# Forget gate's token products in seven blocks of half its columns, with the last steps' weights split into freed places

## The chip, the cores and the metric

The kernel runs on one core of a Trainium2 chip. What counts is the device time of one execution in microseconds (us), lower being better; it is given as the median of several runs.

## The reference

The input x holds 32 slices of 128 tokens with 512 features, all in fp32. Two layers follow one another, each adding to x what a feed-forward part makes of a conditioning part. The first layer's parts are a mixture of experts with a shared expert, and a selection of weights by slice. The second layer's conditioning part sends tokens to 16 experts by a hash of their ids and multiplies the result by a sigmoid gate; its output z enters a gated recurrence over the 32 slices:

```python
def step(c, xt):
    ft = sigmoid(xt @ wf.T + c @ uf.T + bf)
    it = sigmoid(xt @ wi.T + c @ ui.T + bi)
    gt = tanh(xt @ wc.T + c @ uc.T + bc)
    return ft * c + it * gt
# 32 steps, c is 128 x 512; then
h = tanh(z @ wo.T + c_final @ uo.T + bo)
x = x + h
```

All w and u are 512 x 512. The change concerns this recurrence and the step into the last line.

## The kernel before

Every matrix product keeps fp32 accuracy by three products of parts. `split` makes a high part in the format fp32r (a copy on ScalarE, ACT) and a low part (a subtraction on VectorE, DVE) of a tile; `mm3` runs, for each 128 rows of the contraction, high x high, high x low and low x high into one PSUM bank. So a product of 128 x 512 by 512 x 512 is 12 matmuls of 512 moving columns.

A step t of the recurrence has three parts. `from_c` multiplies the state, turned and split into `cT`, by uc, ui and uf: 36 matmuls into three banks of the pool `ps_g`. `gate` adds bias or token product to a bank (DVE, L1720), takes tanh or sigmoid (ACT, L1721); `new_c` forms the new state on DVE (L1726, L1728). `turn` then transposes it on TensorE (tile ptC, L1647) and splits it. The chain from the end of `from_c` of f over the gate, the new state, ptC and the split of `cT` is what the next step waits for; TensorE fills that time with token products of later steps, which need no state.

The token products of c and i are made for two steps at once by Winograd's form of Strassen's product: the tokens of the two steps in two halves of the contraction are A11, A12 (first step) and A21, A22 (second), the weights B11, B21 (wc) and B12, B22 (wi). Seven blocks of 6 matmuls take the place of eight, from the sums S1 to S4 of tokens (`sums_z`, DVE L1637 to L1641) and T1 to T4 of weights. `first_of_pair(n)` runs five blocks and their additions (L1690 to L1695) ahead of the even step 2n, `second_i(n)` one (additions L1705, L1706) and `second_c(n)` one (L1711) ahead of the odd step. A block takes one of the three banks of the pool `ps_b`. In the first two steps `plain` makes the products without sums; there the right half is made from B11, T1 and B22, since T1 has taken the place of B12.

The forget gate's token product is made by `plain` for every step, 12 matmuls of 512 into the same `ps_g` bank to which `from_c` of that step adds; they follow `second_i` in odd steps and `turn` in even ones. Its bias is added by `gate`.

The tokens of step t + 3 are prepared in step t by `gate_y`: a gather of y by GpSimd (POOL, L1587) and a load of r by the queue SP, a sigmoid, a product (L1612), transposes (tile ptF, L1620), a copy, a store of z to DRAM for the last stage, and splits into the tile z. One tile z of two holds the tokens and sums of a pair.

A planner places the instructions of each engine: it takes them in the order written, but where the written one would have to wait, by its own costs, it takes a later one. `issue_after`, `behind` and `queue_behind` hold an instruction back behind another of its engine. A tile in a place used before waits until the old tile's last reader is done.

After the loop the output products come: for 8 groups g of 512 tokens, `unit(g, o)` multiplies wo by the group's z (tile poF, 12 matmuls of 512, four units a group). uo by the final state gives cu (48 matmuls of 128 columns). `result` adds cu, takes tanh, adds x1 and stores. In the old kernel wo is split in step 28, the first group's z and uo behind the loop, while the last step runs.

Pools that matter: `wx_p` holds the split w, `uci` uc and ui, `uf_p` uf, `zp` the tiles z, `zop` raw weights and the sums of blocks, `op` what the last stage loads.

Of the kernel before, what the change touches and what calls it, by code (L numbers as in the profile page):

```python
# [8 lines left out]
F32 = mybir.dt.float32  # L9
# [40 lines left out]
def tile_kernel(ctx: ExitStack, tc: tile.TileContext, a: dict, out: bass.AP):  # L50
# [106 lines left out]
    hl = const.tile([P, KD, NB], F32, name="hl")  # L157
# [18 lines left out]
    with ExitStack() as sa:  # L176
# [653 lines left out]
        new_i = po_p.tile([P, NB], I32, name="new_i")  # L830
        ones = po_p.tile([P, P], F32, name="ones2")
# [734 lines left out]
    with sf:  # L1566
# [35 lines left out]
        zp = sf.enter_context(tc.tile_pool(name="zp", bufs=2, **kw))  # L1602

        zA, zS, zts = {}, {}, {}

        def gate_y(b):
# [6 lines left out]
            if j == 0:  # L1613
                z = zp.tile([P, 2 * KD * D], FR, tag="z", name=f"z_{n}")
                zA[n] = z[:, : KD * D].rearrange("p (j h k q) -> p j h k q", j=2, h=2, k=KD)
                zS[n] = z[:, KD * D :].rearrange("p (s h k q) -> p s h k q", s=4, h=2, k=K2)
                zts[n] = first_p.tile([P, 2, KD, P], F32, tag="cT0", name=f"zt_{n}")
# [5 lines left out]
            zt = zts[n][:, j]  # L1623
            if b < LEAD:
                split(zA[n][:, j, 0], zA[n][:, j, 1], pt)
# [3 lines left out]
            if b >= LEAD:  # L1629
                split(zA[n][:, j, 0], zA[n][:, j, 1], zt)  # L1630

        def sums_z(n):
# [3 lines left out]
            s = gp.tile([P, 2, K2, P], F32, tag="sz", name=f"sz_{n}")  # L1636
# [7 lines left out]
        def turn(c, t):  # L1644
            pt = ps_c.tile([P, KD, P], F32, tag="t", name=f"ptC_{t}")
            for k in range(KD):
                nc.tensor.transpose(pt[:, k, :], c[:, bass.ts(k, P)], ident)  # L1647
# [6 lines left out]

        def block(which, w, n):

            s = {"A11": (0, 0), "A12": (0, 1), "A22": (1, 1)}.get(which)
            if s is None:
                left = zS[n][:, int(which[1]) - 1]
            else:  # L1660
                left = zA[n][:, s[0], :, s[1] * K2 : (s[1] + 1) * K2]
            ps = ps_b.tile([P, D], F32, tag="b", name=f"p{which}_{n}")
            mm3(ps, lambda h, k: left[:, h, k, :], lambda h, k: wt[w][:, h, bass.ts(k, D)], K2)
            return ps

        def plain(t, ps, which, start, stop):
# [5 lines left out]
                "f": ((0, "f0"), (1, "f1")),  # L1672
# [3 lines left out]
            for m, (half, w) in enumerate(todo):  # L1676
                z = zA[n][:, j, :, half * K2 : (half + 1) * K2]
# [6 lines left out]
        half_done, made = {}, []  # L1684

        def first_of_pair(n):

            first, second, c1 = (zop.tile([P, 2, D], F32, tag="raw", name=f"{x}_{n}") for x in ("ta", "tb", "pa"))
            p1, u, v = first[:, 0], first[:, 1], second[:, 0]
            nc.vector.tensor_tensor(p1, block("A11", "B11", n), bias["c"], ALU.add)  # L1690
# [27 lines left out]
        def gate(t, n, ps, v, more):  # L1718
            v[n] = gp.tile([P, D], F32, tag="v" + n, name=f"v_{n}_{t}")
# [5 lines left out]
        def new_c(t, v, c):  # L1725
# [5 lines left out]

        wt = {
            n: wx_p.tile([P, 2, K2 * D], FR, tag="w" + n, name=f"w{n}_hl")
            for n in ("T4", "T3", "T2", "f1", "B22", "T1", "B21", "B11", "f0")
# [26 lines left out]
        for n in "cif":  # L1761
            from_c(0, n, ps, cT, True, False)


        f01 = zp.tile([P, 2 * KD * D], F32, tag="z", name="raw_wf")
        f01 = [f01[:, bass.ts(h, K2 * D)] for h in range(2)]
        with tc.issue_after(first_got):
            for h in range(2):
                nc.gpsimd.dma_start(out=f01[h], in_=a["wf"].rearrange("p k n -> p (k n)")[:, bass.ts(h, K2 * D)])
# [3 lines left out]
        with behind(first_z):  # L1773
            for h in range(2):
                split_part(f"f{h}", f01[h])
# [4 lines left out]
        def rest_of_weights():  # L1780
# [6 lines left out]
            split_part("T4", c1)  # L1787

        cT_next = cT
        for t in range(NB):  # L1790
# [3 lines left out]
            if t == 0:  # L1794
# [3 lines left out]
                with tc.issue_after(done):  # L1798
                    plain(0, ps, "f", False, True)
                for n in "cif":  # L1800
                    gate(t, n, ps, v, more[n])
            else:
                for n in "cif":
# [8 lines left out]
            if t == 0:  # L1812
# [5 lines left out]
                plain(1, ps, "f", True, False)  # L1818
            elif t < NB - 1:
                if odd:  # L1820
                    second_i(n)
                    plain(t + 1, ps, "f", True, False)
                else:
                    first_of_pair(n)
                cT_next = turn(c, t + 1)
                if odd:
                    second_c(n)
                else:
                    plain(t + 1, ps, "f", True, False)
            else:  # L1830
                cT_next = turn(c, t + 1)
            for b in (2, 3) if t == 0 else (t + 3,) if t + 3 < NB else ():
                gate_y(b)
                if b + LEAD < NB:
                    get_y(b + LEAD)
                if b % 2:
# [184 lines left out]
```

## Time and profile before

| what | us |
|---|---|
| median of 3 runs (2414.24 to 2421.07) | 2416.92 |
| the profiled execution | 2416.54 |
| its span in the profile | 2414.9 |
| TensorE busy (PE) | 2393.2 |
| VectorE busy (DVE) | 1485.1 |
| ScalarE busy (ACT) | 1079.8 |
| the recurrence with its start | about 1776 to 2315 |
| one pair of steps in it | 33.2 |
| from its last product to the second group of outputs | 2315 to 2333 |

The granted TensorE clock was 0.999 of full speed. In the profile PE is TensorE's matmuls, PEld its weight loads, which overlap them; L and a number is a line of the kernel, and matmuls of `mm3` all have line 95, so they are told apart by their tiles: ps_c, ps_i and ps_f are the banks of the three gates, pA and pS blocks of tokens and of token sums, poF the output products. A matmul's length in the timeline includes its way through the array, so that neighbours overlap; from one start to the next is its slot. In a row of waits, the engine and tile that waited stand left of the arrow and what ended the wait right of it.

### The profile page before, as it was taken

Reading aid. Unit: us, or ns where it says so; the run is one execution under the profiler, and the core shown is the slowest. Engines: PE = TensorE matmul, PEld = TensorE weight load, DVE = VectorE, ACT = ScalarE, POOL = GpSimd, SP = SyncE. Lnnn points to the kernel's source line nnn. Section 1 sums busy time; section 2 is a strip of 40 time slices with the busy share of each in tenths; the row PEclk is TensorE's granted clock in tenths of the full one; section 3 lists DMA queues with packets and bytes.
Section 4 is the critical chain, followed back from the end, with each engine's and each line's share of the span. In section 5 each row is a group of like instructions: output and inputs, shape, how many; then the busy total and the mean of one; then the engine's idle time right before and its main releaser. Section 6 shows DMA issues by size and latency. Waiting matters only on the chain.

```text
span 2414.9 us, 36797 instructions
## 1 busy us (share of the span) xinstructions
PE 2393.2 (99%) x12792; PEld 2028.2 (84%) x12792; DVE 1485.1 (61%) x2548; ACT 1079.8 (45%) x1897; POOL 417.4 (17%) x461
## 2 busy tenths in 40 slices
PE   9999999999999999999999999999999999999999
PEld 6788888888887888888888889999988888888887
DVE  8797644456567445446455477776756666666664
ACT  5544633343223545445455466666643223223242
POOL 1000022222233233323222120000010000000012
PEclk9999999999999999999999999999999999999999
DMA  6445555457564334343243287677642111111165
GB/s 219 150 131 170 184 171 167 151 188 254 175 222 156 128 128 130 106 132 110 86 151 125 90 297 253 226 224 233 196 156 63 49 44 53 49 44 49 53 238 181
DMA packets 196383, 357.93 MB, mean 148 GB/s; under 512 B 37665, under 2 KB 70481, under 8 KB 193633
## 3 DMA queue, kind: packets, MB, share of 16 engines
q1 hardware_dynamic: 148224, 258.57, 32.0%
q0 software_dynamic: 36448, 75.95, 10.6%
q10 hardware_dynamic: 11520, 20.98, 2.4%
q8 instruction: 107, 1.75, 0.3%
q14 instruction: 84, 0.68, 0.1%
HBM read 377.08 MB, written 91.80 MB: 194 GB/s over the span
## 4 chain that ended last, share of the span: by engine, by line
PE 78%; DMA 1%; DVE 1%; issue 1%; ACT 1%; ACTq 0%; POOL 0%; DVEq 0%; POOLq 0%
PE phD L95 7%; PE poD L95 7%; PE po L95 7%; PE ps_f L95 7%; PE p L95 6%; PE pb L95 4%; PE ps_i L95 4%; PE ps_c L95 4%; PE poF L95 3%; PE pS L95 3%; PE pv L95 3%; PE acc L95 3%; PE pA L95 2%; PE pur L95 2%; PE por L95 2%
## 5 line engine op out<-in xcount | busy, mean ns | idle before, releaser
L65 DVE TENSOR_TENSOR wD<-rawD,wD 128x1024 fp32r<-128x1024 f32 x128 | 156.5, 1229 | 77.6 <-ACT wD L64 77.5
L95 PE MATMUL p<-xhl,swu 128*128 128x512 f32 x768 | 190.6, 400 | 5.7 <-ACT xhl L64 5.7
L95 PE MATMUL p<-xhl,kept_u 128*128 128x512 f32 x768 | 184.6, 394 | 1.2 <-DVE kept_u L65 0.7
L95 PEld LDWEIGHTS phD<-xe,wD 128*128 128x128 f32 x1536 | 183.2, 188 | 1.3
L95 PE MATMUL phD<-xe,wD 128*128 128x256 f32 x1536 | 183.5, 279 | 0.0
L95 PE MATMUL poD<-wD,hD 128*128 128x512 f32 x768 | 181.5, 392 | 0.0
L95 PEld LDWEIGHTS p<-xhl,swu 128*128 128x128 f32 x768 | 145.7, 192 | 36.8 <-ACT xhl L64 5.9
L95 PEld LDWEIGHTS p<-xhl,kept_u 128*128 128x128 f32 x768 | 141.9, 188 | 31.3 <-DVE kept_u L65 1.1
L95 PEld LDWEIGHTS poD<-wD,hD 128*128 128x128 f32 x768 | 141.9, 188 | 28.3
L64 ACT CAST wD<-rawD 128x1024 fp32r<-128x1024 f32 x128 | 133.6, 1047 | 52.7 <-PE poD L95 31.0
L305 POOL DMA_INDIRECT xg<-in_x_rows_dram,blk_t x71 | 68.1, 960 | 439.0 <-PE ptx L315 242.0
L1587 POOL DMA_INDIRECT y<-res_d,gat_i x32 | 35.8, 1118 | 472.9 <-DVE r L1612 394.3
L95 PE MATMUL pur<-r,xb 128*128 x792 | 110.6, 288 | 3.3 <-issue 1.5
L65 DVE TENSOR_TENSOR xb<-ptx,xb 128x512 fp32r<-128x512 f32 x68 | 47.0, 691 | 106.1 <-ACT xb L64 102.7
L95 PE MATMUL por<-r,hbr 128*128 x396 | 107.6, 407 | 0.5 <-ACT hbr L64 0.5
L95 PEld LDWEIGHTS pur<-r,xb 128*128 128x128 f32 x792 | 98.6, 188 | 5.6 <-issue 2.7
L95 PE MATMUL ps_c<-uc_hl,cT 128*128 128x512 f32 x384 | 96.3, 399 | 0.0
L95 PE MATMUL pb<-rT,Wo_hl 128*128 128x256 f32 x768 | 94.7, 281 | 0.3 <-DVE rT L65 0.2
L95 PE MATMUL ps_f<-wf_hl,z 128*128 128x512 f32 x384 | 94.5, 394 | 0.0
L95 PE MATMUL acc<-kept_d,as 128*128 128x512 f32 x384 | 93.6, 392 | 0.4 <-DVE as L65 0.2
L844 POOL DMA_INDIRECT o<-o_d,s_i x64 | 64.7, 1011 | 168.0 <-PE pth L864 82.9
L95 PE MATMUL pv<-w_recept_hl,xr 128*128 128x512 f32 x384 | 93.7, 392 | 0.0
(1048 smaller groups left out, 5130.5 us busy)
## 6 DMA issues: line engine op xcount, KB each, us to landing
rawD<-in_w_key_dram SPq DMA_DIRECT2D x64, 512.0 KB
rawD<-in_w_value_dram SPq DMA_DIRECT2D x64, 512.0 KB
swr<-in_sw_dram SPq DMA_DIRECT2D x120, 256.0 KB
o_d<-obr SPq DMA_DIRECT2D x66, 256.0 KB
rraw<-in_rw_dram SPq DMA_DIRECT2D x32, 256.0 KB
xc<-in_x_dram SPq DMA_DIRECT2D x32, 256.0 KB
hid_d<-o ACTq DMA_DIRECT2D x32, 256.0 KB
xh_d<-xc SPq DMA_DIRECT2D x32, 256.0 KB
```

The costliest lines, as they stand in the source:

```text
L64: first = nc.scalar.copy(hi, src).ins
L65: done = nc.vector.tensor_tensor(lo, src, hi.bitcast(F32), ALU.subtract).ins
L95: done = nc.tensor.matmul(ps, lhsT=left(hl, k), rhs=right(hr, k), start=start and k + n == 0, stop=stop and 3 * k + n == last,)
L305: nc.gpsimd.indirect_dma_start(out=xg[i], out_offset=None, in_=a["x_rows"], in_offset=bass.IndirectOffsetOnAxis(ap=blk_t[:, i : i + 1], ax ...
L844: nc.gpsimd.indirect_dma_start(out=o[n], out_offset=None, in_=o_d, in_offset=bass.IndirectOffsetOnAxis(ap=idx[:, b : b + 1], axis=0),)
L1587: got = nc.gpsimd.indirect_dma_start(out=y, out_offset=None, in_=res_d, in_offset=bass.IndirectOffsetOnAxis(ap=gat_i[:, b : b + 1], axis=0),)
```

## The change

The forget gate's token product also goes by seven blocks, but within one gate: wf is cut into 2 x 2 parts of 256 rows by 256 columns, the tokens of two steps into 2 x 2 parts as before, so the same sums S1 to S4 serve, and the blocks have 256 moving columns. They hold for steps 4 to 31. Steps 0 to 3 use `plain_f`, five half-products of 6 matmuls of 256. The product no longer shares a bank with `from_c`: it goes through `ps_b`, and DVE adds it up in a tile `fs[t]`, into which `gate` then adds `from_c`'s bank. A pair's seven blocks are run as two (`f_start(n + 1)`, in the odd step before the pair), three (`f_first`, behind `turn` of the even step), one (`f_second`, behind `second_i`) and one (`f_third`, behind `second_c`). The adds of `f_start` and `f_second` are queued behind the split of `cT`, those of `f_first` behind the new state.

Places move: the split parts of wf stand in one tile `wf` that begins 64 bytes off a multiple of 512, as the moving operands of the expert stage do (tile xe there, phD the product); the tile z holds tokens alone and the sums have one place `zs`, which raw wf has first; the sums' scratch is the y tile of the odd step, so the gather of the next y comes behind `sums_z`; `hl`, an early tile, leaves the pool `const`.

In the last steps wo is split in step 29 into the places of B11 and B21 (`wo0`), the first group's z in step 30 into those of T1 and T2, and uo behind the final state into uc's. The first group's units use these; wo is split once more, into `wo1`, for the other groups. The transposes of the final state are queued behind `unit(0, 1)`. The second group's z and the first x1 are loaded into ui's place.

```diff
-    hl = const.tile([P, KD, NB], F32, name="hl")
...
+        hl = po_p.tile([P, KD, NB], F32, name="hl")
...
-        zA, zS, zts = {}, {}, {}
+        sz = sf.enter_context(ExitStack())
+        zp = sz.enter_context(tc.tile_pool(name="zp", bufs=2, **kw))
+
+
+        zA, zS, zts, a21 = {}, {}, {}, []
+        BLOCKS = {(0, 0): 0, (0, 1): 1, (1, 1): 2}
+
+        def tokens(n, j, half):
+
+            return zA[n][:, BLOCKS[j, half]] if (j, half) in BLOCKS else a21[0]
...
-                z = zp.tile([P, 2 * KD * D], FR, tag="z", name=f"z_{n}")
+                zA[n] = zp.tile([P, 3, 2, K2, P], FR, tag="z", name=f"z_{n}")
...
-            s = gp.tile([P, 2, K2, P], F32, tag="sz", name=f"sz_{n}")
+            zS[n] = zp.tile([P, 4, 2, K2, P], FR, tag="zs", bufs=1, name=f"zs_{n}")
+            s = spare[2 * n + 1].rearrange("p (s k q) -> p s k q", s=2, k=K2)
...
-            for k in range(KD):
-                nc.tensor.transpose(pt[:, k, :], c[:, bass.ts(k, P)], ident)
+            turned_c[:] = [
+                nc.tensor.transpose(pt[:, k, :], c[:, bass.ts(k, P)], ident).ins for k in range(KD)
+            ]
...
+        def blocks_f(n, *todo):
+
+            ps = ps_b.tile([P, 2, HD], F32, tag="b", name=f"pf{todo[0][0]}_{n}")
+            for i, (which, w) in enumerate(todo):
+                left = left_of(which, n)
+                mm3(ps[:, i], lambda h, k: left[:, h, k, :], lambda h, k: wf[w][:, h, k, :], K2)
+            return ps
...
+        def f_tile(t):
+            pool, tag = (gp, "vf") if t % 2 or t == 0 else (first_p, "c0")
+            fs[t] = pool.tile([P, D], F32, tag=tag, name=f"v_f_{t}")
+            return fs[t][:, :HD], fs[t][:, HD:]
+
+        def plain_f(t):
+            n, j = divmod(t, 2)
+            f_tile(t)
+            ps = ps_b.tile([P, 2, HD], F32, tag="b", name=f"pf_{t}")
+            for i, todo in enumerate((((0, "B11"), (1, "B21")), ((0, "B11"), (0, "T1"), (1, "B22")))):
+                for m, (half, w) in enumerate(todo):
+                    z = tokens(n, j, half)
+                    mm3(
+                        ps[:, i], lambda h, k: z[:, h, k, :], lambda h, k: wf[w][:, h, k, :], K2,
+                        m == 0, m == len(todo) - 1,
+                    )
+            return nc.vector.tensor_tensor(fs[t], ps.rearrange("p i n -> p (i n)"), bias["f"], ALU.add).ins
+
+        def f_start(n):
+
+            f1, p1 = f_tile(2 * n)
+            ps = blocks_f(n, ("A11", "B11"), ("A12", "B21"))
+            return [
+                nc.vector.tensor_tensor(p1, ps[:, 0], bias["f"][:, :HD], ALU.add).ins,
+                nc.vector.tensor_tensor(f1, ps[:, 1], p1, ALU.add).ins,
+            ]
+
+        def f_first(n, room):
+
+            u, v = room[:, :HD], room[:, HD:]
+            p1 = fs[2 * n][:, HD:]
+            ps = blocks_f(n, ("S1", "T1"), ("S2", "T2"))
+            last = blocks_f(n, ("S4", "B22"))
+            with tc.issue_after(made[0]):
+                nc.vector.tensor_tensor(v, ps[:, 0], bias["f"][:, HD:], ALU.add)
+                nc.vector.tensor_tensor(u, ps[:, 1], p1, ALU.add)
+                nc.vector.tensor_tensor(v, v, u, ALU.add)
+                nc.vector.tensor_tensor(p1, last[:, 0], v, ALU.add)
+            f_done[n] = u, v
+
+        def f_second(n):
+            f1, f2 = f_tile(2 * n + 1)
+            u, v = f_done.pop(n)
+            ps = blocks_f(n, ("S3", "T3"))
+            adds = [
+                nc.vector.tensor_tensor(u, ps[:, 0], u, ALU.add).ins,
+                nc.vector.tensor_tensor(f2, ps[:, 0], v, ALU.add).ins,
+            ]
+            return (f1, u), adds
+
+        def f_third(n, f1, u):
+            nc.vector.tensor_tensor(f1, blocks_f(n, ("A22", "T4"))[:, 0], u, ALU.add)
...
+            rooms[n] = second[:, 1]
...
-            v[n] = gp.tile([P, D], F32, tag="v" + n, name=f"v_{n}_{t}")
+            v[n] = fs.pop(t) if n == "f" else gp.tile([P, D], F32, tag="v" + n, name=f"v_{n}_{t}")
...
+        names = ("T4", "T3", "T2", "B22", "T1", "B21", "B11")
+        f_all = shifted(wx_p, len(names) * K2 * D, tag="wf", name="wf_hl")
+        f_all = f_all.rearrange("p (w h k n) -> p w h k n", w=len(names), h=2, k=K2)
+        wf = {n: f_all[:, i] for i, n in enumerate(names)}
         wt = {
             n: wx_p.tile([P, 2, K2 * D], FR, tag="w" + n, name=f"w{n}_hl")
-            for n in ("T4", "T3", "T2", "f1", "B22", "T1", "B21", "B11", "f0")
+            for n in names
...
-            from_c(0, n, ps, cT, True, False)
+
...
+        raw_f = zp.tile([P, KD, D], F32, tag="zs", bufs=1, name="raw_wf")
...
+        f11, f12, f21, f22 = (raw_f[:, h * K2 : (h + 1) * K2, bass.ts(i, HD)] for h in range(2) for i in range(2))
+
+        def split_f(n, raw):
+            split(wf[n][:, 0], wf[n][:, 1], raw)
...
-            for h in range(2):
-                split_part(f"f{h}", f01[h])
+            split_f("B11", f11)
+            split_f("B21", f21)
+            nc.vector.tensor_tensor(f12, f12, f11, ALU.subtract)
+            split_f("T1", f12)
+            split_f("B22", f22)
...
+            nc.vector.tensor_tensor(f22, f22, f12, ALU.subtract)
+            split_f("T2", f22)
+            nc.vector.tensor_tensor(f11, f22, f11, ALU.subtract)
+            nc.vector.tensor_tensor(f21, f21, f22, ALU.subtract)
+            split_f("T3", f11)
+            split_f("T4", f21)
...
-                    plain(0, ps, "f", False, True)
+                    plain_f(0)
+                more["f"] = fs[0]
...
+                more["f"] = fs[t]
...
-                plain(1, ps, "f", True, False)
+                plain_f(1)
             elif t < NB - 1:
                 if odd:
                     second_i(n)
-                    plain(t + 1, ps, "f", True, False)
+
+                    rest, adds = f_second(n) if n > 1 else (None, [])
+                    if n + 1 < NB // 2:
+                        adds += f_start(n + 1)
                 else:
                     first_of_pair(n)
+                    adds = [plain_f(t + 1)] if n == 1 else []
                 cT_next = turn(c, t + 1)
+
+                for i in adds:
+                    queue_behind(i, last_split[1])
                 if odd:
                     second_c(n)
+                    if rest:
+                        f_third(n, *rest)
+                elif n == 1:
+                    plain_f(t + 2)
+                    rooms.pop(n)
+                    b1, b2 = (bias["f"][:, bass.ts(i, HD)] for i in range(2))
+                    nc.vector.tensor_tensor(b2, b2, b1, ALU.subtract)
                 else:
-                    plain(t + 1, ps, "f", True, False)
+                    f_first(n, rooms.pop(n))
             else:
...
             for b in (2, 3) if t == 0 else (t + 3,) if t + 3 < NB else ():
                 gate_y(b)
+                if b % 2:
+                    sums_z(b // 2)
+                spare.pop(b)
                 if b + LEAD < NB:
                     get_y(b + LEAD)
-                if b % 2:
-                    sums_z(b // 2)
             if t == NB - 4:
...
-                wo1 = zp.tile([P, 2, KD, D], FR, tag="z", name="wo_hl")
+                raws = []
...
+                first_z = first_p.tile([P, 2, KD, P], F32, tag="cT0", name="zr_0")
...
+                rest_z = zp.tile([P, 2, KD, P], F32, tag="z", name="zr_0b")
...
+                wo0 = [wx_p.tile([P, 2, K2 * D], FR, tag="w" + n, name=f"wo0_{n}") for n in ("B11", "B21")]
+                for k, raw in enumerate(raws):
+                    part = wo0[k // K2][:, :, bass.ts(k % K2, D)]
+                    split(part[:, 0], part[:, 1], raw)
+            if t == NB - 2:
+                z0 = [wx_p.tile([P, 2, K2 * GT], FR, tag="w" + n, name=f"z0_{n}") for n in ("T1", "T2")]
+                z0 = [z.rearrange("p h (k q) -> p h k q", k=K2) for z in z0]
+                for j, raw in enumerate(first_z):
+                    for i in range(2):
+                        hi, lo = (z0[i][:, h, :, bass.ts(j, P)] for h in range(2))
+                        split(hi, lo, raw[:, i * K2 : (i + 1) * K2])
+                first_z = tuple(last_split)
...
+        def home(g):
+
+            return ((uf_p, "uf"), (op, "zf"), (uci, "uc"), (uci, "ui"))[(g - 1) % 4]
...
+            if g == 0:
+                return mm3(
+                    po, lambda h, k: wo0[k // K2][:, h, (k % K2) * D + o * P : (k % K2) * D + (o + 1) * P],
+                    lambda h, k: z0[k // K2][:, h, k % K2, :], KD,
+                )
...
+        uo1 = uci.tile([P, 2, KD * D], FR, tag="uc", name="uo_hl")
+        came = uci.tile([P, 2, GB, KD, P], F32, tag="ui", name="came")
+        zr[1], x1s[0] = came[:, 0], came[:, 1]
+        for room, d in ((zr[1], z_d[1]), (x1s[0], x1_d[:GB])):
+            nc.sync.dma_start(out=room.rearrange("p b k q -> p b (k q)"), in_=d.rearrange("b p k q -> p b (k q)"))
+        with behind(first_z), tc.issue_after(made[0]):
+            for h in range(2):
+                s = bass.ts(h, K2 * D)
+                split(uo1[:, 0, s], uo1[:, 1, s], raw_part("uo", h))
...
+        ahead = [unit(0, o) for o in range(KD)]
+        sx.close()
+        op = sf.enter_context(tc.tile_pool(name="op", bufs=1, side="right", **kw))
+        wo1 = op.tile([P, 2, KD, D], FR, tag="wo", name="wo_hl")
+        with behind(last_split):
+            for k, raw in enumerate(raws):
+                split(wo1[:, 0, k], wo1[:, 1, k], raw)
+        fetch_z(2)
+        fetch_x1(1)
+        for i in turned_c:
+            queue_behind(i, ahead[1])
...
-                split_z(g + 1)
+                with behind(first_z) if g == 0 else nullcontext():
+                    split_z(g + 1)
```

## The prediction

> **What bounds the kernel now.** I read the page's header first, then the windows of the last stage, the waits of TensorE there, and then the timeline of one pair of steps.
>
> ```profile
> PE 2393.2 (99%) x12792; PEld 2028.2 (84%) x12792; DVE 1485.1 (61%) x2548; ACT 1079.8 (45%) x1897; POOL 417.4 (17%) x461
> ```
>
> A busy TensorE is not yet a full one, so the windows come next. Their columns are length, then busy time of PE, PEld, DVE, ACT and POOL, granted clock, DMA share, GB/s: the start of the recurrence, its first full step, one steady pair of steps, and the change-over to the output products.
>
> ```profile
> 1776.00:1806.00 30.00, 28.75 (x131) 22.96 (x130) 12.57 (x16) 13.02 (x18) 9.30 (x11) 1.00 0.53 175
> 1806.00:1826.00 20.00, 19.96 (x92) 16.09 (x91) 18.92 (x28) 9.61 (x15) 1.16 (x1) 1.00 0.22 67
> 2053.42:2086.62 33.20, 33.20 (x155) 27.47 (x155) 20.81 (x33) 9.86 (x16) 2.28 (x2) 1.00 0.16 48
> 2315.03:2332.80 17.77, 17.09 (x102) 14.80 (x101) 14.15 (x24) 10.45 (x21) 0.00 (x0) 1.00 0.77 280
> ```
>
> A steady pair takes 33.2 us and PE has no gap in it. The PE waits from 1860 to 2315 us form an empty list; the only one from 2315 us on is
>
> ```profile
> PE ptC L1647 <- DVE c L1728: 0.7, 1, 0.7
> ```
>
> So in the recurrence only two things can shorten the time: fewer PE slots, and that last wait. What a slot costs is read from the chain of waits, which lists runs of equal matmuls without gaps:
>
> ```profile
> 1755.88 11.31 PE phD L95 x96
> 1767.19 10.93 PE poD L95 x48
> 2186.26 4.08 PE pS L95 x18
> ```
>
> phD has 256 moving columns: 11.31/96 = 0.118 us a slot (0.1177 in the earlier stretches of 11.30). The blocks pS have 512: 4.08/18 = 0.2267. Half the columns cost 0.519 of the whole, not 0.5.
>
> **The change part by part.** *Forget products, pairs 2 to 15 (14 pairs).* Removed: 2 steps x 12 matmuls of 512 = 24 x 0.2267 = 5.44 us. Added: 7 blocks x 6 matmuls of 256 = 42 x 0.1177 = 4.94 us. That is -0.50 us a pair, -7.0 in all.
>
> *Forget products, steps 0 to 3.* plain_f needs five half-products of 6 matmuls (two for the left columns, three for the right, since the right half of wf is held as T1 and added back): 30 x 0.1177 = 3.53 us instead of 12 x 0.2267 = 2.72. +0.81 x 4 = +3.2 us. Sum on PE: -3.7 us, which is on the path because PE is full.
>
> The page "TensorE: Matmul & The Clock Gate", section "Back-to-back issue gap", gives N/2.4 + 2.5 ns for a matmul alone, 109 and 216 ns; by it the two terms would be -8.3 and +2.7, a sum of -5.6. Its table "Why this matters for your kernels" asks for all dimensions of 512 or more, which speaks against halving the columns. The rows show 118 and 227, so the measured pair decides.
>
> *Evictions.* Before, the token product stayed in the bank of ps_f; now nine 256-wide adds a pair go to DVE. The nearest row is the 128x256 add of the token sums, 0.42 us long, 0.34 from one to the next (1819.55 to 1819.89); 128x512 adds take 0.69 from PSUM as from SBUF. So 3.1 to 3.8 us a pair on top of 20.8 of 33.2: DVE stays at some 24.5 of 32.7. Hidden by PE, as long as none stands ahead of the chain c -> cT. The adds of f_start and f_second are queued behind cT's split, those of f_first behind the new c; what that does to the banks is the first rival.
>
> *The chain in an odd step.* These rows show one (the columns are start, length, then the instruction):
>
> ```profile
> 2069.19 1.52 PE L95 MATMUL pS<-wT_hl,z 128*128 128x512 f32 x6
> 2070.55 2.88 PE L95 MATMUL ps_f<-wf_hl,z 128*128 128x512 f32 x12
> 2071.51 0.69 DVE L1728 TENSOR_TENSOR c<-v_f,v_i 128x512 f32<-128x512 f32 x1
> 2072.72 0.68 DVE L1706 TENSOR_TENSOR pd<-pS,tb 128x512 f32<-128x512 f32 x1
> 2073.27 0.60 PE L1647 MATMUL ptC<-ident,c 128*128 128x128 f32 x4
> 2074.53 0.69 DVE L65 TENSOR_TENSOR cT<-ptC,cT 128x512 fp32r<-128x512 f32 x1 [1.13 <-ACT cT L64]
> ```
>
> Ahead of ptC PE now runs 6 x 0.2267 + 18 x 0.1177 = 3.48 us instead of 4.08, so it is there at 2072.67. c is added by 2072.20, and at the end of the scan ptC followed the end of that add by 0.15 (2320.26 to 2320.41): ready at 2072.35. The cover shrinks from 0.9 to 0.3 us, and no stall follows; if it were gone, each 0.1 us would cost 1.4 us in all. Behind ptC stand 1.36 + 0.71 + 0.48 (ptF) = 2.55 us against the 1.95 that cT's split takes from ptC on. In an even step 6.8 us stand ahead of ptC as before, and 2.12 + 0.48 behind it instead of 3.2: still more than 1.95.
>
> *Start.* Between 1806 and 1826 us DVE is busy 18.92 of 20, and v_c of step 1 is added at 1816.21 although its product was done by 1812.4: DVE is 3.8 us behind. The change adds there three subtractions and three splits of wf's blocks (6 x 0.60) and two adds of fs (1.2), 4.8 us. The token sums of pair 1 cannot be written before raw_wf is used up, since both take the one place "zs". What PE has in hand against it: its own 2 x 0.81 more in steps 0 and 1, and 7 us of plain_f(2) and plain_f(3) that need neither sums nor c. Bounds: 0 (all covered) and 4.8 - 1.6 = 3.2 us; I take 1.0, near the lower end, because 7 us of products that need no sums are at hand. In step 0 the two splits of 1024 (1.23 each on DVE) become four of 512 and a subtraction, 0.6 more; the 1.25 us that PE stands idle in the first window are waits for gathered rows and what hangs on them, which nothing here touches: 0, or at best -0.3.
>
> *The last steps.* wo, the first tokens and uo are split into places of wx_p while PE is full, and the final ptC is put behind unit(0,1). Before, the sigmoid of v_i stood behind zF's casts on ACT; the 19 matmuls of poF that went ahead had filled 2315.26 to 2319.57, and ptC came at 2320.41, 0.84 us later. Now 24 matmuls (5.44 us from 2315.03) stand ahead of ptC, and the chain of 3 us is done first: -0.8 us. If the split of uo came late it would be given back: its 1 MB takes 2.8 us at the 380 GB/s that the DMA view of 2290 to 2345 us shows at its busiest, against 10 us until cu. wo is now split twice (wo0 for the first group, wo1 for the rest): four splits of 0.69 more on DVE, which after the last c (2318.2) has uo 2.5, cT 0.7, wo1 2.8 and z1 2.8 us to do until the second group at 2331.7, so 4 us are to spare; a later one would cost what it is late. The token tile z1 now waits for the place of ui (free at 2312.3), and is wanted at 2332: 19 us for 2 MB, no cost.
>
> *Queues.* get_y(b+2) of an odd b moves behind the sums, since they now use y's place; POOL's gather goes some 16 us later (2065.5 to 2081.3) and is wanted 16 us after that (next odd r product at 2097.8). Only the next gather stands behind it on POOL, at 2081. SP's load of r goes with it and is still a step early. hl's move is 512 bytes of place: 0.
>
> Sum: -7.0 + 3.2 - 0.8 + 1.0 = -3.6 us. Against the profiled execution's 2416.54 (span 2414.9 and 1.6 around it; 0.4 under the median of the runs) that is 2413.0.
>
> **The rivals.** *First: a wait for a PSUM bank takes back the gain.* ps_b has three banks. In an odd step S3T3, f_second and f_start take all three in 3.48 us. second_c needs one: S3T3's is free when L1706 ends (2073.40 in the rows), but PE is past ptC at 2073.15. f_third needs the next, which f_second frees only after its two adds behind cT's split: 2074.62 + 0.34 + 0.42 = 2075.4, where PE would be at 2074.8. In written order that is 0.3 + 0.6 = 0.9 us a pair; if ptF goes ahead of second_c, 0.4; if ps_c of the next step also goes ahead of f_third, nothing. Times 14: +5.6 to +12.9, hence 2418.6 to 2425.9. It decides from 0.26 us a pair on, where the gain is gone. For it: the spare is one bank fewer than in the rows. Against it: the order here is a planned one, not the written one; in the first steps products for c and i stand interleaved, and around 1823 half of ps_f was put between two blocks of pS, with 0.2 us lost to a bank. A plan that sees the bank late will put other products first. This is the end on the slower side.
>
> *Second: the start costs its upper bound.* +3.2 instead of 1.0 gives 2415.2: no change to be seen. For it speaks that DVE is 95% busy there; against, the 7 us of other products.
>
> *Third: everything covered.* Start 0, step 0 -0.3: 2411.7. To be faster by 7.2 us no PE slots are left in the sum; only the spread between runs could show it.
>
> The sentence of "Trainium Kernel Development and Optimization", section "Best Practices", to mind PSUM pressure because evictions don't get faster with the products, points to the first rival; this trace shows such a wait only at 1823 us, 0.2 us long.
>
> **How the numbers follow.** No wait in the steady pairs: 0.70, of which 0.58 the forecast, 0.07 the second rival and 0.05 the third. A bank wait in every pair: 0.24, spread evenly over its prices. A cost in the steady pairs that I have not found, with nine more adds on DVE and twelve tiles a pair through three banks: 0.06. The time is the forecast's, 2413.0. The runs lay from 2.7 below to 4.2 above their median, so the forecast alone is 2410 to 2417. The range goes from 2409 (the third rival less the spread of runs) to 2423, past the middle of the first rival. About what a measurement can tell from no change is 0.3%, 7.25 us: slower by more than that takes 0.78 us a pair, the last quarter of the first rival (0.07), the unknown cost (0.06) and a little of the spread, 0.16 in all; faster by more has only the spread and what I have overlooked, 0.10; 0.74 lies between.
>
> **What would show it.** The window of a steady pair should be 32.7 us long with PE without a gap; ps of the f blocks should appear as 42 matmuls of 128x256 at 0.118 us. L1728 -> ptC should be gone from the PE waits after 2315 us. The first rival shows as PE waits of pf or pA on DVE, 14 times, and as a pair over 33.0 us; the second as PE waits between 1815 and 1850 us. I am wrong if the 256-wide matmuls of f take over 0.13 us (their gain is then nil: 5.44/42), or if a stage ahead of 1776 us moves.

## The result, and the profile after

The changed kernel takes 2422.24 us (median of 20 runs, 2420.26 to 2427.99), the kernel before in the same comparison 2417.01 (2412.52 to 2421.07): ratio 1.0021, 95% interval 1.0015 to 1.0027. It is slower by 5.2 us where 3.6 us less were forecast; the time lies within the stated range, but on the other side of the kernel before. The profiled execution of the changed kernel has a span of 2420.7 us. Its header:

```profile
PE 2393.5 (99%) x13116; PEld 2039.4 (84%) x13116; DVE 1535.6 (63%) x2697; ACT 1080.9 (45%) x1911; POOL 415.7 (17%) x461
```

TensorE has 324 more slots and the same busy time. The windows (length, then busy time of PE, PEld, DVE, ACT, POOL, granted clock, DMA share, GB/s) are again the start, the first full steps, a steady pair and the change-over; the recurrence begins 4 us later in this execution.

```profile
1780.00:1810.00 30.00, 28.92 (x147) 24.03 (x146) 14.17 (x21) 13.23 (x21) 8.35 (x10) 1.00 0.48 166
1810.00:1832.00 22.00, 19.29 (x104) 15.43 (x103) 20.98 (x32) 11.74 (x19) 1.28 (x2) 1.00 0.17 50
2037.04:2069.91 32.87, 32.87 (x176) 28.04 (x173) 23.83 (x43) 9.56 (x16) 2.29 (x2) 1.00 0.16 48
2321.06:2338.70 17.64, 17.12 (x103) 14.97 (x101) 13.16 (x20) 8.99 (x18) 0.00 (x0) 1.00 0.82 304
```

The pair is 32.87 us instead of 33.20, without a gap, and DVE is at 23.83 of it. But the second window has 2.7 us without PE, while DVE is busy 20.98 of 22. The waits of TensorE from 1800 to 2345 us (in total, times, longest):

```profile
PE ptC L1667 <- DVE c L1816: 2.5, 1, 2.5
PE cu L95 <- ACT cu L2059: 0.5, 1, 0.5
PE ps_c L95 <- ACT cT L64: 0.3, 1, 0.3
PE pS L95 <- DVE zs L65: 0.2, 1, 0.2
```

The last ptC's wait of before (0.7 us) is gone as foretold. A ptC of the first steps now waits 2.5 us, and at the change-over cu, the product of uo by the final state, waits 0.5 us on ScalarE. In the timeline of VectorE (start, length, instruction) the reason for the first is to be read:

```profile
1818.50 1.22 DVE L65 TENSOR_TENSOR wT_hl<-raw_wc,wT_hl 128x1024 fp32r<-128x1024 f32 x1
1819.64 0.68 DVE L1890 TENSOR_TENSOR raw_wf<-raw_wf 128x512 f32<-128x512 f32 x1
1820.24 0.68 DVE L1891 TENSOR_TENSOR raw_wf<-raw_wf 128x512 f32<-128x512 f32 x1
...
1821.44 1.28 DVE L65 TENSOR_TENSOR wf_hl<-raw_wf,wf_hl 128x512 fp32r<-128x512 f32 x2
...
1823.92 0.68 DVE L1808 TENSOR_TENSOR v_c<-ps_c,bc_bc 128x512 f32<-128x512 f32 x1
...
1829.73 0.68 DVE L1816 TENSOR_TENSOR c<-v_f,v_i 128x512 f32<-128x512 f32 x1
```

The subtractions and splits for wf's blocks stand ahead of step 1's gates (v_c), and the new c comes at 1830.4. On TensorE the products that could have covered this stand behind the waiting transposes, in the queue's order:

```profile
1826.78 1.20 PE L95 MATMUL pS<-wT_hl,zs 128*128 128x512 f32 x4 [0.23 <-DVE zs L65]
1830.46 0.66 PE L1667 MATMUL ptC<-ident,c 128*128 128x128 f32 x4 [2.48 <-DVE c L1816]
...
1833.94 3.70 PE L95 MATMUL pf<-wf_hl,z 128*128 128x256 f32 x30
```

The chain of work of one steady pair shows where the pair's gain is short (start, length, run of matmuls): four transposes of the tokens, ptF, are cut in two around pA.

```profile
2146.12 1.41 PE pfA L95 x12
2147.53 0.44 PE ptC L1667 x4
2147.97 0.22 PE ptF L1627 x2
2148.19 1.62 PE pA L95 x6
2149.81 0.22 PE ptF L1627 x2
2150.03 0.47 PE ps_c L95 x2
```

The list above has TensorE's matmuls only. The weight loads have waits of their own; from 1880 to 2300 us the kernel before has none, and the changed kernel has

```profile
PEld pA L95 <- DVE pd L1794: 2.6, 13, 0.2
```

once in each pair. One of them in the timeline:

```profile
2114.55 0.68 DVE L1794 TENSOR_TENSOR pd<-pS,tb 128x512 f32<-128x512 f32 x1
2114.94 0.38 PE L1627 MATMUL ptF<-ident,r 128*128 128x128 f32 x2
2115.28 1.23 PEld L95 LDWEIGHTS pA<-wT_hl,z 128*128 128x128 f32 x6 [0.20 <-DVE pd L1794]
2115.29 1.66 PE L95 MATMUL pA<-wT_hl,z 128*128 128x512 f32 x6
```

The add pd (L1794, in `second_i`) reads the bank of S3T3, and pA, the block of `second_c`, starts as soon as that add is done.

To tell the change's own part from the rest I cut each profile at the first product with the state (the first ps_c from uc, 1777.9 before and 1781.9 after). Ahead of it both kernels issue the same instructions in the same order on every engine. From there to the end ("the stretch") the profile before has 636.9 us, the one after 638.8: 1.9 us of the 5.2. So there were four questions: the 0.16 us missing from each pair, the start, the cu wait, and 3.3 us which no wait of this profile shows.

### The profile page after: what moved, and what is told of

The parts are those of the page before. It is cut to its first block, busy times and chain, and to the rows that moved or that the text cites. A ratio compares the mean times of both kernels' runs of the same rounds, so it can differ in the third digit from the quotient of the medians.

```text
span 2420.7 us, 37653 instructions
## 1 busy us (share of the span) xinstructions
PE 2393.5 (99%) x13116; PEld 2039.4 (84%) x13116; DVE 1535.6 (63%) x2697; ACT 1080.9 (45%) x1911; POOL 415.7 (17%) x461
## 3 DMA queue, kind: packets, MB, share of 16 engines
q10 hardware_dynamic: 11520, 20.98, 2.4%
## 4 chain that ended last, share of the span: by engine, by line
PE 77%; DVE 2%; DMA 2%; issue 1%; ACT 1%; ACTq 0%; POOL 0%; SPq 0%; DVEq 0%; POOLq 0%
PE phD L95 7%; PE po L95 7%; PE poD L95 7%; PE p L95 5%; PE pb L95 4%; PE ps_i L95 4%; PE ps_c L95 4%; PE poF L95 4%; PE ps_f L95 3%; PE pS L95 3%; PE pv L95 3%; PE acc L95 3%; PE pA L95 3%; PE pur L95 2%; PE por L95 2%; PE pfS L95 2%
## 5 line engine op out<-in xcount | busy, mean ns | idle before, releaser
L95 PE MATMUL acc<-swd,as 128*128 128x512 f32 x384 | 94.5, 391 | 0.5 <-ACT as L64 0.3
```

Source lines behind the costliest of these rows:

```text
L95: done = nc.tensor.matmul(ps, lhsT=left(hl, k), rhs=right(hr, k), start=start and k + n == 0, stop=stop and 3 * k + n == last,)
```

## The experiments

**Is the early part slower?** The kernel before once more, and the kernel before with only hl moved as the change moves it:

```diff
-    hl = const.tile([P, KD, NB], F32, name="hl")
...
+        hl = po_p.tile([P, KD, NB], F32, name="hl")
```

> The kernel of before once more, unchanged, for where its recurrence begins. In the two profiles the first matmul of ps_c that follows the last poD stands 3.96 us later after the change than before it (1782.1 against 1778.1 us from the span's start), although both engines' orders up to there are the same. Theory U (the early part is really slower, because tile hl lies elsewhere and all tiles behind it 512 bytes lower): this run begins its recurrence at 1778, within 1 us, like the first one. Rival N (it is the spread from one execution to the next): it lies anywhere between 1776 and 1783 us.

> The kernel of before with one part of the change: hl moved from const to po_p. Nothing else differs; all tiles behind hl lie 512 bytes lower, as after the change. Theory U: 2420.5 us or so, +3 to +4 on before, ratio 1.0012 to 1.0017, with the recurrence beginning at 1781 to 1783 us. Rival N: ratio 1.0000 within 0.0006, and the recurrence begins at 1776 to 1780.

Measured: the repeated kernel before has its first product with the state at 1782.1 instead of 1777.9 us and a stretch of 636.5. One and the same kernel's early part thus varies by 4 us between executions. With hl moved: 2416.53 us, ratio 0.9995 (0.9986 to 1.0004), early part 1779.6, stretch 636.9. No cost of hl's place is seen, and the profiles' 4 us say nothing of the change.

**The pair's missing gain.** The changed kernel with second_c and f_third traced behind the tokens' transposes:

```diff
                 if odd:
-                    second_c(n)
-                    if rest:
+                    if t + 3 >= NB:
+                        second_c(n)
                         f_third(n, *rest)
...
                 gate_y(b)
+                if t and odd:
+                    second_c(n)
+                    if rest:
+                        f_third(n, *rest)
```

> The changed kernel, with second_c and f_third traced behind gate_y in odd steps, so that the four transposes ptF stand together again. In the changed kernel a pair of steps takes 32.87 us where 32.71 was reckoned, and ptF stands as two and two around the block A22. Theory: the 0.16 us are the price of going once more from transposes to products, so the pair takes 32.71 here and the time falls by 13 x 0.155 = 2.0 us, to 2420.2 (ratio to before 1.0013). Rival: the 0.16 us are the wait for S3T3's bank, which then shows elsewhere; pair 32.8 to 32.9, time 2422.

Measured: a pair takes 32.70 us (32.87 in the changed kernel), the stretch 636.7; 2421.72 us, ratio to before 1.0013 (1.0004 to 1.0022). Its chain in the same place:

```profile
2145.46 0.44 PE ptC L1667 x4
2145.90 0.44 PE ptF L1627 x4
2146.33 1.40 PE pA L95 x6
2147.73 0.46 PE ps_c L95 x2
```

pA behind undivided transposes takes 1.40 instead of 1.62 us. The pair's length is the one that the theory names, but the cause is the rival's: a wait for the bank of S3T3. In all 13 pairs of the changed kernel the first matmul of pA starts 0.055 us after the end of the add pd, and 0.24 us after the start of the transpose before it; here the second figure is 0.03, as it also is in the changed kernel from ptF to ps_c, so a change from transposes to products does not bring such a gap by itself. Two transposes ahead of pA cover only part of the wait for the bank, four cover it. It isn't in the list of PE's waits because a transpose's record, 0.27 us long, reaches past pA's start. The weight loads' list of this kernel has pA no longer, but the next bank instead, that of `f_second`:

```profile
PEld pfA L95 <- DVE v_f L1747: 2.6, 13, 0.2
```

Of this about 0.05 us a pair reach PE: pfA's second matmul starts 0.163 instead of 0.118 us after its first. The price of the 256-wide slots was right.

**The start.** The changed kernel with the splits that only step 4 needs (wf's T2, T3 and T4) put behind step 2's state; the raw weights get the place of wc's T4, whose split goes with them:

```diff
+        raw_f = wx_p.tile([P, KD, D], F32, tag="wT4", name="raw_wf")
...
-            split_part("T4", c1)
+
+        def rest_of_f():
             nc.vector.tensor_tensor(f22, f22, f12, ALU.subtract)
...
             split_f("T4", f21)
+            wt["T4"] = wx_p.tile([P, 2, K2 * D], FR, tag="wT4", name="wT4_hl")
+            split_part("T4", c1)
...
+                if t == 1:
+                    with behind(tuple(last_split)):
+                        rest_of_f()
```

> The changed kernel, with wf's parts T2, T3 and T4 made and split behind the state of step 2 instead of behind that of step 1; raw wf lies in the place of T4 until then (which is split last), so that the token sums of the first pair don't wait for it. Theory: in the changed kernel DVE has these six (3.6 us) ahead of step 1's gates, ptC of step 2 waits 2.5 us for the new state, and the wait is gone here; the time falls by 2 to 3 us, to 2419.7 (ratio 1.0011), with PE waits of under 0.6 us between 1810 and 1845 us. Rival: DVE is behind by more than these, the wait stays over 1.5 us, and the time falls by less than 1 us.

Measured: 2417.16 us, ratio to before 0.9997 (0.9988 to 1.0006), so the loss is gone. The wait of ptC is no longer in the list; the stretch is 635.4, that is 3.4 us less than in the changed kernel, of which 2.5 are the wait. The ratio fell by more than that, 0.0024 or 5.8 us; the clock, below, accounts for most of the rest. Two things differ here at once: c comes 2.0 us earlier after the first product with the state (46.5 instead of 48.5), and the planner now put step 2's forget product ahead of ptC, so that 3.5 us of products stand there:

```profile
1828.79 3.70 PE L95 MATMUL pf<-wf_hl,z 128*128 128x256 f32 x30
1832.33 0.60 PE L1667 MATMUL ptC<-ident,c 128*128 128x128 f32 x4
```

What each of the two would do alone was not run.

**The cu wait, and all of it together.** The changed kernel once more, then with the casts of the third group behind the last eviction of cu, then with all three alterations:

```diff
-            nc.scalar.activation(cu[:, o, :], pc, AF.Identity, bias=bo1[:, o : o + 1])
+            cu_done = nc.scalar.activation(cu[:, o, :], pc, AF.Identity, bias=bo1[:, o : o + 1]).ins
...
-                with behind(first_z) if g == 0 else nullcontext():
+                with behind(first_z) if g == 0 else tc.issue_after(cu_done):
                     split_z(g + 1)
```

> The changed kernel once more, unaltered, so that it stands beside the other kernels on the same chip. From the first product with the state (the first matmul into ps_c) to the end of the span its profile had 638.8 us, the kernel before 637.0. That is 1.9 of the 5.2 us by which the medians differ; 3.3 us lie ahead of the recurrence, where both kernels issue the same instructions in the same order. Theory V (the early part only varies from one execution to the next, and the medians of the first comparison fell apart by chance): the stretch is again 638.8 within 0.3, and the median lies some 2 us above that of the kernel before, ratio 1.0008. Theory R (the changed program's early part is itself slower, by some 3 us): the stretch is the same, and the median again lies 4 to 6 us above, ratio 1.0017 to 1.0025.

> The changed kernel with one order changed on ScalarE: the casts of the third group's tokens (zF) are issued behind the last eviction of cu instead of ahead of its second one. Theory (the changed kernel took away the wait of the last ptC and paid for it with a new one, cu behind the casts, 0.5 us in the profile and 0.69 with what hangs on it): the wait of cu on ScalarE is gone, the stretch from the first product with the state to the end is 638.1 instead of 638.8 us, and the median is 0.7 us below the changed kernel's in this job, which is less than the intervals of these medians. Rival (the group's tokens are then late): the first product of the third group waits for zF, and the stretch stays at 638.8 or above.

> The changed kernel with three alterations at once: the splits of three of wf's parts behind step 2's state (the stretch was 3.4 us shorter by this alone), the second half of the pair's products for c and f traced behind the tokens' transposes (2.1 us shorter alone), and the zF casts behind the last eviction of cu (0.7 expected); besides, step 3's forget product reads its own pair's first half of tokens, which costs one more split of 128x256 off the path. If the three add up, the stretch from the first product with the state to the end is 638.8 - 3.4 - 2.1 - 0.7 = 632.6 us, 4.4 below the kernel before's 637.0. Theory V (the early part is the same but for its variation): the median is 4.4 us below the kernel before, ratio 0.998. Theory R (the changed program's early part is slower by some 3 us): 1 to 2 us below, ratio 0.9994. If the steady pairs lose again what the start gives, the stretch stays over 634 us.

Measured, against 2419.06 for the kernel before in this comparison: the changed kernel 2424.91, ratio 1.0024 (1.0015 to 1.0034); casts behind cu 2421.61, 1.0013 (1.0004 to 1.0022), the cu wait gone; all three 2414.99, 0.9984 (0.9975 to 0.9992). The last is faster than both kernels; its stretch is 633.1 us where the three alone would give 632.6. The loss of the changed kernel was thus there again, as theory R has it, but not where R puts it: the early part is 1782.8, and the stretch is 642.0 instead of 638.8 with the same waits. What differs is the granted clock. The records of its clock show two pieces of 3.41 us at half clock inside the stretch, one behind the wait of ptC, one behind that of cu; if each makes 3.41/2 = 1.7 us of delay, 642.0 - 3.4 = 638.6 is left. The cast's order brought 3.3 us where 0.7 were expected, again more than the wait itself.

**What does a wait do to the clock?** The combined kernel with a delay between c and its transposes in 12 odd steps, once (below) and four times (range(4)):

```diff
             c = new_c(t, v, c)
+            if t % 2 == 0 and 6 <= t < 30:
+                for _ in range(1):
+                    made[:] = [nc.vector.tensor_scalar(c, c, 1.0, None, ALU.mult).ins]
```

> The combined kernel (deferred splits, tokens' transposes after the state's, casts behind cu), with one more multiplication of the new state by 1.0 on VectorE in 12 odd steps of the steady pairs (pairs 3 to 14): 0.69 us more on the way from c to ptC. TensorE's order is the same. In these steps ptC starts 0.47 us after the end of c's add in the combined kernel and 0.15 is the least seen, so 0.32 us are spare: a wait of 0.37 us should open in each, 12 x 0.37 = 4.4 us in all. Theory C (a wait of TensorE can be followed by 3.4 us at half the granted clock, which costs another 1.7 us; seen behind 2 of 4 waits of 2.5 us and 1 of 4 of 0.5 us): stretches at half clock appear in the steady pairs, between 2 and 8 of them, the mean clock falls by 0.001 to 0.006, and the time rises by 8 to 18 us against the combined kernel's 2415. Rival (the dips come from somewhere else, and a wait costs its length): the clock stays at 1.00 throughout the steady pairs and the time rises by 4.4 us, to 2419.4.

> The same with four such multiplications, 2.77 us more on the way from c to ptC, in the same 12 steps. On TensorE the 4 transposes of the tokens now stand ahead of ptC (0.48 us), the rest is in the same order: a wait of 2.77 - 0.32 - 0.48 = 2.0 us in each, and some 0.16 us for one more change between transposes and products, 26 us in all. Theory C: half of the waits or more are followed by 3.4 us at half clock, 6 to 12 times 1.7 us, so the time rises by 36 to 46 us and the mean clock falls by 0.004 to 0.009. Rival: 26 us, with the clock at 1.00.

Measured: with one multiplication a pair takes 33.11 us instead of 32.70 and the stretch 637.4, 4.3 us more than the combined kernel's 633.1 (the rival has 4.4); 2420.02 us, ratio to before 1.0014 (1.0005 to 1.0024). With four: stretch 658.3, 25.2 more (the rival has 26); 2439.72 us, ratio 1.0088 (1.0071 to 1.0104). With one multiplication no wait of PE is listed; the delay shows again in the weight loads, where pA waits 0.3 us for the add pd in 12 pairs, so no wait of 0.37 us at ptC came about. Waits and window (clock in the third column from the right) with four:

```profile
PE ptC L1667 <- DVE c L1920: 11.0, 12, 0.9
PE pS L95 <- DVE ta L1778: 3.5, 10, 0.5
PE ps_c L95 <- ACT cT L64: 2.6, 11, 0.2
```

```profile
1914.00:2300.00 386.00, 368.42 (x1901) 308.68 (x1899) 275.80 (x510) 104.88 (x178) 23.05 (x20) 1.00 0.15 46
```

TensorE stands 17.6 us in 386, and the clock stays at 1.00. Theory C falls in the form in which I had put it: in these profiles waits of up to 0.9 us among 512-column products cost their length and no more. But instead of one wait of 2.0 us in each step there are three, at ptC, pS and ps_c, of 0.9 us at most, so a wait as long as that of the start was not tried here. The mean granted clock of the timed runs is 0.9992 in both kernels, 0.9996 in the kernel before beside them, so that a piece in a few of the other executions isn't excluded.

**Where the half clock comes from.** The changed kernel twice more and the kernel before, each once:

> The changed kernel once more, for its granted clock alone. So far the half-clock stretch of 3.41 us near 100 us (behind 32 products of 16x16, long before the changed code) stood in 4 of 4 profiles of kernels with the changed start (the 2.5 us wait of ptC) and in 1 of 7 others, and the one behind the wait of ptC in 2 of 4. Theory P (where the clock's 3.41 us windows fall is chance, the same for every kernel): the stretch near 100 us is there in about half of the profiles, this one and the kernel before alike. Theory K (it is tied to the kernel): it stands in this profile and in the next, and not in that of the kernel before. Behind the ptC wait near 1828 us both expect a half-clock stretch if 2.0 us or more of the wait fall into one window of the 3.41 us grid that the clock's records show, and none if 1.6 or less do.

> The same kernel a second time, with the same expectations; the grid's place is another draw.

> The kernel before, unaltered. Theory P: a half-clock stretch near 100 us with a chance of about one half. Theory K: none. Both: none between 200 and 2300 us, since no wait there is over 1.4 us long.

Measured: no half clock near 100 us in any of the three, so theory K falls; that place had it in 5 of 14 profiles, of four different kernels. In the stretch the kernel before has none again (636.6 us). The changed kernel has three pieces in one profile and two in the other. The windows of the first of them, on the grid that its clock records show:

```profile
1825.70:1829.11 3.41, 1.15 (x4) 0.63 (x4) 3.41 (x7) 0.62 (x2) 0.15 (x1) 1.00 0.00 0
1829.11:1832.53 3.42, 3.19 (x10) 2.71 (x11) 2.58 (x5) 0.59 (x1) 1.94 (x2) 0.50 0.32 85
2334.28:2337.70 3.42, 2.90 (x27) 2.76 (x26) 2.18 (x4) 2.53 (x6) 0.00 (x0) 1.00 0.90 299
2337.70:2344.53 6.83, 6.83 (x23) 5.86 (x24) 6.13 (x10) 5.25 (x11) 2.88 (x2) 0.50 0.48 128
```

In the window ahead of the first piece PE worked 1.15 of 3.41 us, 2.26 of the wait fell into it, and the next window runs at 0.50. In the first profile of the changed kernel the same wait was shared by two windows, the fuller of them

```profile
1828.84:1832.25 3.41, 1.79 (x9) 1.42 (x10) 3.41 (x7) 0.59 (x1) 1.53 (x2) 1.00 0.09 13
```

with 1.62 us without PE, and the clock stayed. Over the six profiles with this wait the fuller window has 2.27, 2.26, 2.19 and 2.16 us without PE, each followed by half clock (in the third, 0.22 us of it are the wait of pS just before); 1.62 and 1.58, neither. In the profile with the deferred splits a window of 1.84 us without PE near 1404 us was not followed by it either. Among these windows the limit lies between, and the two that were run for it fell on the side that the expectation had given.

Behind the cu wait of 0.52 us half clock followed in 3 of 6 profiles (once for two windows), and in none of the 8 without that wait at this place. There PE runs products of only 128 columns. On the grid of the records, the 3.41 us ahead of each of the 13 half-clock windows of the 14 profiles (those after the last product left out) have matmuls of 1536 to 3584 moving columns in all, where such a window has 7424 as a rule; this is so behind the ptC wait, behind the cu wait and near 100 us. Yet 31 other windows had 3584 or fewer and no half clock behind them. So few columns go with the half clock at all three places, but do not decide it, and what does stays open.

## Why the prediction was wrong, by its own terms

Stretches by profile, the half-clock loss taken out of the last column (us):

| kernel | profiles | stretch | half-clock loss | stretch without it |
|---|---|---|---|---|
| before | 3 | 636.9, 636.5, 636.6 | 0 | 636.7 |
| changed | 4 | 638.8, 642.0, 643.4, 642.0 | 0, 3.4, 5.1, 3.4 | 638.6 |
| tokens' transposes whole | 1 | 636.7 | 0 | 636.7 |
| deferred splits | 1 | 635.4 | 0 | 635.4 |
| casts behind cu | 1 | 639.5 | 1.7 | 637.7 |
| all three | 1 | 633.1 | 0 | 633.1 |

The means of before and changed differ by 641.6 - 636.7 = 4.9 us, nearly all of the 5.2 of the medians: 1.9 in order and waits, 3.0 in half clock. The timed runs agree. Their mean granted clock is 0.9983 for the changed kernel and 0.9994 for the kernel before (67 runs of the later comparisons), 0.0011 x 2420 = 2.7 us. It is 0.9983 with the tokens' transposes whole, where both waits stay, 0.9990 with the casts behind cu, where only that of ptC stays, 0.9992 with the deferred splits, where only that of cu stays, and 0.9995 in the combined kernel, where both are gone. So the half clock comes with these two waits and goes with them.

- *Forget products of the pairs, -7.0.* The slots were priced rightly (0.118 us), the sum was not: 33.21 - 32.87 = 0.34 a pair, -4.8. The step that failed is the forecast's own, "no wait in the steady pairs". The first rival had it right: pA waits for S3T3's bank in every pair. Its size was smaller than the prices given there (0.4 and 0.9 us; the upper one times 14 is 12.6, not 12.9), since the plan put two of the four transposes ahead: 0.17 us. With all four ahead the pair gave 33.21 - 32.70 = 0.51, the predicted 0.50.
- *Steps 0 to 3, +3.2.* 120 slots of pf took 14.2 us against 48 x 0.2267 = 10.9: +3.3.
- *Start, +1.0 of 0 to 3.2.* Waits of 2.7 us, plus 0.75 windows of half clock on average, 1.3: 4.0, above the upper bound. The step that failed: the "7 us of products that need no sums" cover a wait only if they stand ahead of the waiting instruction. pf of steps 2 and 3 stood behind ptC. The second rival was the true case here, and it weighed more than it was given.
- *Last steps, -0.8.* The wait of ptC went, as foretold, and the 0.5 us of cu on ScalarE came in its place. From the first output product to the end of the span: 99.6 us before, 99.5 after, -0.1. Behind it half clock, one window on average: +1.7. The step that failed: I had followed VectorE's new splits there and not ScalarE's casts.
- *Last odd step, 0.* The cover that I had put at 0.3 us was 0.32 in the steady pairs (ptC 0.47 us after c against a least of 0.15). In the last pair, without f_start's products, it was gone: the list has 0.3 us for ps_c, 0.6 with the slots lengthened around it.
- *DVE, queues, hl, step 0:* at nothing, as predicted; DVE is at 23.8 of 32.87.

Sum of the measured terms without the clock: -4.8 + 3.3 + 2.7 - 0.1 + 0.6 = +1.7 against 1.9 measured; 0.2 stays unassigned. Of the 8.8 us between forecast and result the clock is 3.0, the bank 2.2, the start's waits 1.7, the change-over 0.7 and the last odd step 0.6.

The clock was in no term. The Trainium skill, "TensorE: Matmul & The Clock Gate", section "What's actually happening", tells of a free-running window of 3413 ns, after which the array's clock is halved or released. The records here show 3.41 us and 0.50. The same section puts the throttle behind an idle window, and the page's section "HAM oscillation — how this bites in real kernels" warns of gaps over about 3.4 us. Here a window with 1.15 us of work was enough, behind a gap of 2.5 us, so the rule taken at its word would have missed it.

## What to carry to other kernels

Work that is at hand covers a wait only if it stands ahead of the waiting instruction in its engine's queue: look in the order, not in the sum. A short wait for a bank can be missing from the waits of the matmuls: look at the weight loads' too. A wait of TensorE that fills most of a clock window (here 2.2 of 3.41 us) is charged twice, its length and then half of the next window, and only in some executions; so price it with the mean granted clock of many runs, and don't trust one profile. Slots are the safe part of a sum: here they were right to a few hundredths of a us a pair once the bank's wait was covered, and what was lost was lost in waits and in the clock that followed them.

## What the runs showed of the hardware that I had not expected

The half-clock pieces are 3.41 us or two times that, on a grid that runs through the whole execution, and the same wait of 2.48 us costs nothing more or 1.7 us more by where it falls on it. A wait of 0.52 us among products of 128 columns was followed by half clock in 3 of 6 profiles, twelve of 0.9 us among products of 512 columns in none. The early 1780 us of one unchanged kernel varied by 4 us between executions.
